# Neighbourhood attention beside a state space layer: layer 1's first block prepared in two steps a turn, and the quotients moved behind the product with the tables

## The chip, the cores and the metric

The kernel runs on one core of one Trainium2 chip. A core has five engines that work side by side, each through its own queue in order: PE (TensorE, matrix products), DVE (VectorE), ACT (ScalarE), POOL (GpSimd) and SP (SyncE, which here only issues DMA transfers). The metric is the time of one execution on the device in microseconds.

## The reference

Four layers work on an input of 4 images of 56 x 56 positions and 128 channels, all in fp32; each adds its result to its input. The change lies at the end of layer 0 and the beginning of layer 1.

```python
# layer 0: attention over a 7 x 7 neighbourhood, 4 heads of 32 channels, on group-normalised x
attn = jnp.einsum('bnijd,bnipjqd->bnijpq', q, k_win) + bias[None]
attn = jax.nn.softmax(attn.reshape(B_, nh, H_, W_, k * k), axis=-1)
out = jnp.einsum('bnijpq,bnipjqd->bnijd', attn, v_win)
return out @ w_proj + b_proj

# layer 1: two Mamba blocks on group-normalised x, over sequences of 56 positions
u = jax.nn.silu(conv(u) + cb)                      # four taps
dt, Bm, Cm = jnp.split(u @ xw, [DT_RANK, DT_RANK + D_STATE], axis=-1)
delta = jax.nn.softplus(dt @ dtw + dtb)
h = exp(delta * A) * h + delta * u * Bm            # the scan, 16 states a channel
y = sum(h * Cm) + u * D
return (y * jax.nn.silu(res)) @ ow
```

Layer 2 is an additive attention with a mixture of 64 experts behind it, layer 3 a softmax attention with a mixture of 8 experts. The change doesn't touch their code.

## The kernel before

**Layer 0.** An image is cut into 7 chunks of 8 rows (448 positions), so there are 28 chunks, numbered k from 0. Each chunk is done in two units, one for each group of column bands, so there are 56 units. A loop with a turn for each unit, and five turns more at the end, writes out the order of PE, ACT, DVE and POOL by hand. Turn i issues:

- the scores of unit i + 1 on PE (`scores`, L510), after them the steps kept in the lists `early` and `turns`;
- the weights of unit i + 1 (`weights`): exp on ACT out of PSUM (L522), then the product with the tables of the position bias (L527), three heads on DVE and one on POOL;
- the steps kept in `mid`, then the sums of unit i - 1 on PE (`sums`, L540), which gather both numerators (o) and denominators (d) of a chunk in two PSUM buffers of one copy each;
- the steps kept in `at`.

Every chunk's own work is dealt to these lists: query (`queries`, L461 and L466), key (`keys`, L471 and L475), values in two halves (`values`, L485 and L492), and the end of the chunk, `finish(k)`, in four steps. `copied` moves d and o from PSUM to SBUF on ACT (L557) and adds the projection's bias to x on POOL (L558). `divided(0)` and `divided(1)` take the reciprocal of one half of d each (L562) and multiply oT with it (L563), on DVE. `projected` is four products on PE (L568) and the sum to x on DVE (L571). The buffer d has one copy, oT two. With "end" the first turn after the chunk's own two, `copied` and `divided(0)` are in `at` of turn end, `divided(1)` in `at` of turn end + 1, `projected` in `early` of turn end + 3:

```python
for n, to, step in zip((0, 0, 1, 3), (at, at, at, early), finish(k)):
    add(end + n, step, to=to)
```

Nearly all small products (query, key, values, projection, transpositions) share one ring of two PSUM buffers, `m`; a product waits until what was there two products before has been moved out.

**The next image's norm** (`norm_steps`) is dealt over the first 12 turns of an image: seven transpositions with their statistics (L228, L238), the groups' mean and root (L245 to L273), and normalising on DVE (L285).

**Layer 1's first block.** In the last image (turns 42 to 55) the same places are taken by `next_norm`, 21 steps: seven transpositions of image 0 with statistics (n = 0 to 6), four steps to mean and root (7 to 10), `place` (11), which transposes and normalises one chunk into a room that layer 0 no longer uses (L291), and nine steps of the first Mamba block (12 to 20): two convolutions of four products each (L1012), the gate's two products (L1074) with Silu (L1025), the product with `xw` (L1031), four products that spread its rows (L1042), Softplus (L1056), the product of delta and u on POOL (L1060), and eight writes of delta and du to DRAM (L1067). The moves from PSUM are on ACT (L1020, L1082, L1037, L1048, L1053). Steps 0 to 6 come two to a turn, steps 7 to 20 one to a turn, in turns 46 to 59.

**Layer 1.** The states of 8 channels by 16 lie on the 128 partitions. SP reads delta back from DRAM, spread over the states (`fetch`, tile E, L825), ACT takes its exp (L844), PE spreads du (L806), DVE multiplies (L853) and scans (L860), POOL multiplies by C (L865), PE sums the states (L871). There are 896 scans. The tiles of layer 1 lie where tiles of layer 0 lay; a fetch waits until those are read.

Of the kernel before, what the change touches and what calls it, by code (L numbers as in the profile page):

```python
# [25 lines left out]
NCH = S // CH  # L26
# [112 lines left out]
class Hybrid:  # L139
# [215 lines left out]
    def layer0(self, wp1):  # L355
# [5 lines left out]
        with ExitStack() as ctx:  # L361
# [64 lines left out]
            def next_norm():  # L426
                g = self.first_norm = self.group_norm(0, wp1, group)
                parts = g.groups(m)
                chunk = lambda c: lambda: (g.turn(c, m), g.stats(c))
                both = lambda fs: lambda: [f() for f in fs]  # L430

                def place():
                    self.hold_block()
                    rows = self.du_room[:, : SEQ * (DC - 1 + HW)].rearrange(
                        "p (s t) -> p s t", t=DC - 1 + HW
                    )
                    nc.gpsimd.memset(rows[:, :, : DC - 1], 0.0)
                    g.chunk = lambda c: rows[:, :, DC - 1 :]
                    g.turn(0, m)
                    g.scaled(0, g.ps)  # L440
                    self.h[0, 0, 0] = rows

                s = self.first_block = self.mamba_pre(0, (0, 0, 0), None, m)
                conv = lambda f: lambda: ([s.conv(f, k) for k in range(DC)], s.conved(f))
                return [
                    *[chunk(c) for c in range(NCH)],
                    parts[0], both(parts[1:3]), both(parts[3:5]), parts[5], place,
                    conv(0), conv(1), lambda: (s.res(0), s.resed(0), s.silu("us")),
                    lambda: (s.res(1), s.resed(1)), lambda: (s.xproj(), s.dbl()),
                    lambda: (s.spread(0), s.parts(0)), lambda: (s.spread(1), s.parts(1)),  # L450
                    lambda: (s.spread(2), s.spreaded(0), s.delta()),
                    lambda: (s.du(), s.spread(3), s.spreaded(1)),
                ]
# [93 lines left out]
            def finish(k):  # L547

                b, c = chunks[k]
                x = self.X[b][:, TC * c : TC * (c + 1), :]  # L550
                r = {}

                def copied():
                    r["o"], r["d"] = self.t(sm, [P, CH], "oT"), self.t(sm, [P, CH], "d", bufs=1)
                    ps = dict(zip("od", out.pop(k)))
                    for n in "do":
                        nc.scalar.copy(r[n], ps[n][:, :CH])  # L557
                    nc.gpsimd.tensor_add(x, x, bproj.unsqueeze(1).to_broadcast([TP, TC, C]))  # L558

                def divided(n):  # L560
                    own = slice(n * 2 * TP, (n + 1) * 2 * TP)
                    nc.vector.reciprocal(r["d"][:, own], r["d"][:, own])  # L562
                    nc.vector.tensor_mul(r["o"][:, own], r["o"][:, own], r["d"][:, own])  # L563

                def projected():
                    ps = m().rearrange("p (k c) -> p k c", c=C)
                    for i in range(TC):
                        nc.tensor.matmul(  # L568
                            ps[:TP, i, :], r["o"][:, i * TP : (i + 1) * TP], wproj, start=True, stop=True
                        )  # L570
                    nc.vector.tensor_add(x, ps[:TP], x)  # L571

                return [copied, lambda: divided(0), lambda: divided(1), projected]
# [31 lines left out]
            at, mid, early, turns = {}, {}, {}, {}  # L605
            add = lambda i, f, *args, to=at: to.setdefault(i, []).append(lambda: f(*args))
# [4 lines left out]
                    add(first[NCH * (b - 1)] + n, step, to=turns if n < NCH else at)  # L611
            for n, step in enumerate(next_norm()):
                i = first[NCH * (B - 1)]
                add(i + n // 2 if n < NCH else i + n - 3, step, to=at if n % 2 and n < NCH else mid)
            for k, (b, c) in enumerate(chunks):
                i = first[k]
                end = first.get(k + 1, len(units))
                for n, to, step in zip((0, 0, 1, 3), (at, at, at, early), finish(k)):
                    add(end + n, step, to=to)
                if k >= 3:  # L620
                    add(first[k - 1] - 2 if c == 1 else first[k - 3] + (1 if c else 3), keys, k)
                if k + 1 < len(chunks):
                    add(max(i - 1, 0), queries, k + 1)
                    for half in range(2):
                        add(i + half, values, k + 1, half, to=mid)
# [1581 lines left out]
```

## Time and profile before

| What | Value |
|---|---|
| Runs of the kernel | 7031.51 us median of 3 (7016.09 to 7035.77) |
| The profiled execution's own time | 7027.59 us |
| Its span, first to last instruction | 7025.8 us |
| Busy in the span: PE, DVE, ACT, POOL | 6054.1, 5763.3, 4832.9, 2849.9 us |
| Layer 0's loop, first to last scores | 40.9 to 364.5 us |
| First scan of layer 1 | 392.1 us |
| Last scan of layer 1 | starts at 2968.0 us |
| Mean granted clock of TensorE | 0.931 |

A line of the profile's timeline gives the start in us, the duration, the engine, the line of the kernel, the operation, the tile written and the tiles read, their shapes, a count where several are merged, and in brackets how long the engine had been idle and what ended that. An entry `PE m L568` after an arrow is the instruction that was waited for. PEld is the loading of weights, which overlaps with products. A table by stages gives for each stretch its length, each engine's busy time with its number of instructions, the granted clock of TensorE, the busy share of the DMA engines and the GB/s that they moved.

### The profile page before, as it was taken

What the parts mean: (1) busy time and instruction counts of PE and PEld (TensorE: products, weight loads), DVE (VectorE), ACT (ScalarE), POOL (GpSimd) and SP (SyncE); (2) the same over time, 40 slices, a digit from 0 to 9 for tenths busy, and PEclk for the clock granted to TensorE, in tenths of its full rate; (3) what the DMA queues carried; (4) which work ended last, traced back from release to release, by engine and by line L of the source; (5) the groups of instructions that cost most, each with busy time, mean ns of one, the idle gap of its engine ahead of it and who ended that gap; (6) DMA issues with size and microseconds to landing.
All of it is one profiled execution on the core that took longest, in us unless ns stands there. A gap on an engine that the chain in (4) does not pass through costs nothing.

```text
span 7025.8 us, 101491 instructions
## 1 busy us (share of the span) xinstructions
PE 6054.1 (86%) x37386; PEld 2622.7 (37%) x37386; DVE 5763.3 (82%) x10108; ACT 4832.9 (69%) x4828; POOL 2849.9 (41%) x1921
## 2 busy tenths in 40 slices
PE   8889999999999999877777777777788799999998
PEld 7633333333233233232233323332333355555554
DVE  6879999999999999977878888888887753566665
ACT  5567667776766777589989998999899833322231
POOL 2369989998999999811010001000101100000000
PEclk9989989999999899889999999999899999999999
DMA  3057767777776777600000000000003304243433
GB/s 53 5 139 187 187 165 186 184 178 175 188 185 171 176 189 187 153 8 3 1 6 3 8 2 6 4 6 3 6 20 116 89 18 149 72 109 92 118 85 94
DMA packets 363447, 654.19 MB, mean 93 GB/s; under 512 B 95413, under 2 KB 211909, under 8 KB 362438
## 3 DMA queue, kind: packets, MB, share of 16 engines
q1 hardware_dynamic: 362949, 647.71, 36.9%
q8 instruction: 295, 4.83, 0.3%
q14 instruction: 203, 1.66, 0.1%
HBM read 536.78 MB, written 104.37 MB: 91 GB/s over the span
## 4 chain that ended last, share of the span: by engine, by line
PE 23%; ACT 12%; DVE 11%; issue 8%; POOL 1%; SPq 0%; DMA 0%; DVEq 0%; ACTq 0%; POOLq 0%
ACT th L1306 10%; PE o L1944 6%; DVE th L1297 6%; PE q L1932 5%; PE s L1320 5%; DVE X L2144 2%; PE pe L2139 2%; ACT e L1334 1%; POOL e L1341 1%; PE o L1350 1%; PE m L1478 1%; PE m L1253 1%; DVE wide L1964 1%; DVE X L1486 0%; PE m L1761 0%
## 5 line engine op out<-in xcount | busy, mean ns | idle before, releaser
L1306 ACT ACTIVATE th<-th 128x5488 f32<-128x5488 f32 (+13 forms) x560 | 2184.2, 3943 | 175.4 <-DVE th L1297 151.4
L1297 DVE TENSOR_SCALAR th<-fT,g 128x784 f32<-128x784 f32 (+13 forms) x3920 | 1868.9, 549 | 307.2 <-PE s L1320 286.5
L1320 PE MATMUL s<-th,place 128*32 128x392 f32 (+5 forms) x14112 | 1391.6, 488 | 442.2 <-ACT th L1306 439.5
L860 DVE TENSOR_TENSOR_SCAN hs<-E,u 128x896 f32<-128x896 f32 x728 | 1449.7, 2007 | 3.6 <-ACT E L844 3.6
L844 ACT ACTIVATE E<-E,rate 128x448 f32<-128x448 f32 x1456 | 886.0, 661 | 121.9 <-DMA E<-delta_dram 118.4
L865 POOL TENSOR_TENSOR hs<-hs,room 128x896 f32<-128x896 f32 x448 | 924.8, 2083 | 82.9 <-DVE hs L860 82.5
L865 POOL TENSOR_TENSOR hs<-hs,bc 128x896 f32<-128x896 f32 x448 | 926.5, 2087 | 47.3 <-DVE hs L860 45.6
L1320 PEld LDWEIGHTS s<-th,place 128*32 128x32 f32 (+1 forms) x14112 | 455.1, 111 | 1311.1 <-ACT th L1306 666.3
L1937 ACT ACTIVATE e<-q,shift 128x448 f32<-128x448 f32 (+1 forms) x511 | 322.0, 633 | 673.7 <-PE q L1932 653.4
L1341 POOL TENSOR_TENSOR e<-e,later 112x112 f32<-112x112 f32 x112 | 155.0, 1384 | 1131.4 <-ACT e L1334 676.6
L2144 DVE SCALAR_TENSOR_TENSOR X<-pe,r_gate,X 112x128 f32<-112x128 f32 x896 | 311.9, 348 | 309.6 <-PE pe L2139 273.5
L871 PE MATMUL y<-hs,sum 128*32 128x448 f32 x3584 | 499.4, 631 | 4.0 <-POOL hs L865 4.0
L1932 PE MATMUL q<-xT 128*128 128x448 f32 (+1 forms) x1022 | 501.3, 573 | 0.9 <-ACT e L1937 0.9
L1944 PE MATMUL o<-e,xk 128*128 128x448 f32 (+1 forms) x1022 | 479.2, 552 | 16.1 <-ACT oT L1909 16.1
L806 PE MATMUL u<-room,pick 32*128 32x448 f32 x1456 | 413.4, 638 | 68.5 <-DVE hs L860 66.7
L1350 PE MATMUL o<-e,xk 112*128 112x392 f32 (+5 forms) x1024 | 389.3, 500 | 91.8 <-POOL e L1341 88.2
L806 PE MATMUL u<-du,pick 32*128 32x448 f32 x1456 | 402.8, 618 | 74.2 <-DVE hs L860 72.9
L1237 POOL MEMSET xa<- 112x4 f32 (+1 forms) x32 | 55.1, 1723 | 969.9 <-PE m L1230 969.8
L853 DVE TENSOR_TENSOR u<-u,bc 128x896 f32<-128x896 f32 x364 | 391.8, 1076 | 26.1 <-PE u L806 25.8
L853 DVE TENSOR_TENSOR u<-u,room 128x896 f32<-128x896 f32 x364 | 391.8, 1076 | 22.0 <-PE u L806 21.9
L2073 POOL MEMSET lc_xa<- 112x4 f32 x28 | 3.1, 109 | 945.7 <-DVE lc_xa L2067 696.4
L848 ACT ACTIVATE u<-u 128x896 f32<-128x896 f32 x168 | 151.9, 904 | 297.3 <-PE u L797 218.1
(310 smaller groups left out, 8767.5 us busy)
## 6 DMA issues: line engine op xcount, KB each, us to landing
E<-delta_dram SPq DMA_DIRECT2D x728, 448.0 KB
V<-du_dram SPq DMA_DIRECT2D x168, 448.0 KB
wide<-in_L_ffn_weight SPq DMA_DIRECT2D x64, 1024.0 KB
r<-M SPq DMA_DIRECT2D x189, 224.0 KB
M<-wide SPq DMA_DIRECT2D x72, 392.0 KB
du_dram<-room SPq DMA_DIRECT2D x112, 112.0 KB
delta_dram<-room SPq DMA_DIRECT2D x112, 112.0 KB
du_dram<-du SPq DMA_DIRECT2D x112, 112.0 KB
```

What stands on the lines that cost most here:

```text
L806: nc.tensor.matmul(halves(to)[:, k], w["pick"][own, q, :], pre[j]["du"][own, f], start=True, stop=True,)
L844: nc.scalar.activation(e, e, AF.Exp, scale=rate)
L853: eng.tensor_mul(v, v, pre[p // PAIRS]["bc"][:, 0:1].to_broadcast([P, 2, CH]))
L860: nc.vector.tensor_tensor_scan(flat, E.pop(p), V.pop(p), 0.0, op0=ALU.mult, op1=ALU.add)
L865: nc.gpsimd.tensor_mul(HS[p], HS[p], bc[:, 1:2].to_broadcast([P, 2, CH]))
L871: nc.tensor.matmul(py[j, f][r * HD : (r + 1) * HD, :], w["sum"][:, q, :], HS[p + r // 2][:, r % 2], start=False, stop=(q == QG - 1),)
L1297: nc.vector.tensor_scalar(th[i][:, s, lo:hi], fT[j][:, lo:hi], g[b, J // WT][:, at : at + 1], None, op0=ALU.add,)
L1306: nc.scalar.activation(own, own, AF.Tanh)
L1320: nc.tensor.matmul(ps[j, J][QW * blk : QW * blk + rows, h, lo:hi], place[:, off : off + rows], z[:, at + s, h * HALF + lo : h * HALF + hi] ...
L1350: nc.tensor.matmul(po[j][:, h, lo:hi], xk[b, J // WT][:, J % WT, :], e[:, h * HALF + lo : h * HALF + hi], start=(J == 0), stop=(J == t + ( ...
L1932: nc.tensor.matmul(ps[:n, :CH], of_tile(xT[b], t), xT[b][:, c * CH : (c + 1) * CH], start=True, stop=True,)
L1944: nc.tensor.matmul(po[b, c], xk[b][:n, t, :], e[:n], start=first, stop=last)
```

## The change

All of it is where steps are put into the lists of turns. Steps 7 to 20 of layer 1's first block follow the first seven at two to a turn: even ones in `mid`, odd ones in `at`, in turns 45 to 52. And `divided(0)` goes from `at` of turn end to `mid` of turn end + 1, `divided(1)` from `at` of turn end + 1 to `mid` of turn end + 2. `copied` and `projected` keep their places. In `mid` of the last image's turns, steps of `next_norm` stand ahead of `divided`, in `at` ahead of `copied`.

```diff
             for n, step in enumerate(next_norm()):
                 i = first[NCH * (B - 1)]
-                add(i + n // 2 if n < NCH else i + n - 3, step, to=at if n % 2 and n < NCH else mid)
+                add(i + n // 2, step, to=at if n % 2 else mid)
             for k, (b, c) in enumerate(chunks):
                 i = first[k]
                 end = first.get(k + 1, len(units))
-                for n, to, step in zip((0, 0, 1, 3), (at, at, at, early), finish(k)):
+                for n, to, step in zip((0, 1, 2, 3), (at, mid, mid, early), finish(k)):
                     add(end + n, step, to=to)
```

No instruction is added to or taken from the program but what the places imply: the order on each engine, the waits, and on ACT the loads of function tables between functions of different sets.

## The prediction

> **What bounds the kernel now.** I read the table of busy time by stage first. The three stretches are a middle piece of layer 0, loop turns 46 to 53, and the passage into layer 1.
>
> ```profile
> core 0: us, PE busy (x) PEld busy (x) DVE busy (x) ACT busy (x) POOL busy (x), PEclk, DMA share, GB/s
> 200.00:280.00 80.00, 69.83 (x1370) 55.92 (x1366) 63.68 (x86) 47.89 (x79) 31.04 (x21) 0.99 0.02 6
> 318.56:363.97 45.41, 43.06 (x798) 32.96 (x797) 32.07 (x40) 30.61 (x47) 17.40 (x13) 1.00 0.01 3
> 363.97:392.10 28.13, 24.13 (x246) 13.14 (x242) 14.32 (x16) 13.14 (x20) 7.00 (x7) 0.88 0.28 71
> ```
>
> In layer 0, PE works 87% and then 95% of the stretch: it is the bound, and what counts is what it waits for. Its waits come from the timeline. This is one pair of turns, from one even scores product (L510) to the next, with the same place of the following pair last:
>
> ```profile
> 234.94 0.86 PE L510 MATMUL s<-q,kT 32*112 32x112 f32 x24
> ...
> 237.34 1.21 DVE L527 TENSOR_TENSOR e<-e,tab 112x1008 f32<-112x1008 f32 x1 [0.34 <-ACT e L522]
> ...
> 238.93 0.54 ACT L557 COPY d<-d 128x448 f32<-128x448 f32 x1
> ...
> 239.47 1.13 PE L568 MATMUL m<-wproj,oT 128*112 128x128 f32 x8
> 239.50 1.55 DVE L562 RECIPROCAL d<-d 128x224 f32<-128x224 f32 x1 [0.94 <-ACT d L557]
> ...
> 241.66 0.68 DVE L571 TENSOR_TENSOR X<-m,X 112x512 f32<-112x512 f32 x1
> ...
> 242.41 0.91 PE L485 MATMUL m<-wqkv,room 128*112 128x128 f32 x6 [1.43 <-DVE X L571]
> ...
> 246.68 0.86 PE L510 MATMUL s<-q,kT 32*112 32x112 f32 x24
> ...
> 252.16 0.82 PE L485 MATMUL m<-wqkv,room 128*112 128x128 f32 x6
> ```
>
> The projection (239.47) waits for nothing. Its sum (241.66) sits on DVE behind the next chunk's quotient (239.50), and PE waits 1.43 us for it, because a transposition stands between projection and values and the two-buffer ring m comes round. In the next pair nothing stands between, and values start at once (252.16). At the image's last turns another wait shows:
>
> ```profile
> 285.39 0.54 ACT L557 COPY d<-d 128x448 f32<-128x448 f32 x1
> ...
> 286.23 0.66 ACT L475 ACTIVATE kT<-m,bqkv 128x448 f32<-128x448 f32 x1
> ...
> 286.94 1.09 PE L510 MATMUL s<-q,kT 32*112 32x104 f32 x32 [1.02 <-ACT kT L475]
> ```
>
> The next image's first scores wait for keys that ACT moves only behind the denominators' copy. Last, the passage:
>
> ```profile
> 363.97 0.86 PE L510 MATMUL s<-q,kT 32*112 32x112 f32 x24
> ...
> 382.51 0.34 SPq L1067 DMA_DIRECT2D du_dram<-room  x1
> ...
> 386.40 1.29 SPq L825 DMA_DIRECT2D E<-delta_dram  x2
> ...
> 390.84 1.23 ACT L844 ACTIVATE E<-E,rate 128x448 f32<-128x448 f32 x2 [6.97 <-DMA E<-delta_dram]
> ...
> 392.10 2.02 DVE L860 TENSOR_TENSOR_SCAN hs<-E,u 128x896 f32<-128x896 f32 x1 [1.76 <-ACT E L844]
> ```
>
> From the last unit's scores to layer 1's first scan are 28.1 us; from 500 us on DVE is busy 59.5 of 60 us. So a later or earlier scan shifts the end by as much.
>
> **What the Trainium skill says.** PSUM — Partial Sum Buffer, "Engine vs sequencer instructions": the queues of ScalarE, VectorE and GpSimdE are strict FIFO. The trace agrees: the kT copy at 286.23 stands behind the d copy. ScalarE: Activation LUTs, "What ACT_TABLE_LOAD costs", states about 1283 ns for a load and more for a drain; the trace has 1.28 us, with the next function 1.3 us after the load's start, so I price 1.3. TensorE: Matmul & The Clock Gate, "What's actually happening": an idle PE falls to half clock. The trace agrees: four L1012 take 3.35 us at 381.94 and 1.77 at 386.48. SBUF — State Buffer, "SBUF: two separate sides", says that a GpSimd instruction and a DVE one with two SBUF inputs block each other for a whole instruction. The trace agrees: the same table product takes 2.31 us at 314.16, with POOL's part running from 313.99 for 1.06, and 1.54 at 219.28, after POOL's had ended. So part of DVE's sums can come 0.8 us later than I count.
>
> **The change, part by part.** T is the start of an even scores product; durations are the trace's.
>
> *Quotients.* The number of instructions stays. In order of DVE it was: table product, first half of quotient k, sum k-1, table product, second half. It becomes: table product, second half of k-1, sum k-1, table product, first half of k. What is late next:
>
> (a) The second half of the projection now needs exp (ends T+2.3), table product (T+2.4 to 3.6), reciprocal and product (1.94): T+5.55. PE gets there at T+4.5 and fills 0.55 with the first half. It resumes at 5.65, and behind it on PE stand values, sums, query and key; the sum ends at 7.0; values with a transposition before them start at 7.05 instead of 7.47: -0.4. There are 7 such pairs: -2.8. Without a transposition values start at T+6.2 and not 5.48: +0.75, in 3 pairs: +2.25. The pair with the statistics' second matmul, which waited for the sum too (265.10), breaks even.
>
> (b) d has one buffer. Copying denominators k on ACT must now wait for the second half of k-1: T+5.6, not T+4.0. Behind it on ACT stand the copy of oT, the next exp and the moves of v and q. In a plain pair exp then ends at 8.4 instead of 6.6, while the next scores come at 11.7: hidden; with less than 3.3 us of cover each us would cost one. At the image's end it is not hidden: DVE is behind with normalising (1.88 and 1.44). Counting DVE from 271.3: 1.95 quotient, 5.0 root and normalising, 0.4, 0.7 sum, 1.55, 1.95, 1.44, 0.4, table product to 285.8, second half to 287.75. Copies d and oT to 288.9, kT to 289.55: scores at 289.6 instead of 286.94: +2.7, three times: +8.1.
>
> (c) In turns 42 to 45 of the last image two transpositions fall in a turn. Half a quotient now stands between two statistics that free m: 15.0 instead of 13.1 us and 13.4 instead of 12.35: +2.9.
>
> *First block.* 14 steps move from turns 46 to 59 into turns 45 to 52. PE: two convolutions of 3.2, two L1074 of 0.9, L1031 1.77, four L1042 of 1.0. Of these 6.7 us came behind the last scores and now come ahead of them. ACT: the moves of these products (0.55 to 0.65 each), Silu 0.96, Softplus 0.95, and one more return to the exp table, 1.3. POOL: 2.07 + 0.3, in turn 52; its 17.4 us busy of 45 hide it (otherwise 2.4). SP: eight writes, 3.6 us, on a queue that is idle there; the fetches behind them wait for buffers of layer 0 anyway. I set the durations one behind another in queue order:
>
> - Turns 46-47 take 15.9 us (before 11.15). The square root waits for the second statistics behind a quotient (6.5); then copies 1.1, exp table 1.3, exp to 10.85, table product to 12.5, root to 14.1, the normalised chunk to 14.9. Keys need its m buffer: to 15.85.
> - Turns 48-49: 18.3 (before 9.66). PE alone: 9.4 of usual work with key and query, 6.5 and 1.8 of the block; the wait for m behind Silu and its table is 0.65.
> - Turns 50-51: 15.9 (before 12.11). PE 13.3: 8.5 of usual work, 1.8 and three times 1.0; then scores wait 2.6 for q, which stands on ACT behind the move of bc, table and Softplus (12.4 to 15.2), then 0.65.
> - Turns 52-53: 9.5 (before 12.49): 7.6 without key and query, 1.0, and 0.75 to 0.9 of wait (a).
>
> Together 59.6 against 45.4: +14.2.
>
> *Passage.* From the last scores: table product to 3.6, second half of 25 to 5.55, copies of 26 to 6.7, sum 25 to 7.0, quotient 26 to 10.9, copies of 27 to 12.05, sum 26 to 12.3, quotient 27 to 16.2, projection and sum to 17.7. First convolution and spread inputs to 18.7, again to 20.6, two DVE products to 21.8: scan. E, fetched once the last sums end (9.6) and landing 4.4 later as before, is there by 14. At half clock the scan comes at 25.7; I take 23.8: -4.3. The five first scans spread over 15.8 us before, as PE stood behind a move that waited on ACT for E (392.64 after 386.48). With E there I count 11.3 at full clock; half clock eats about 1: -3.5.
>
> Sum: -2.8 + 2.25 + 8.1 + 2.9 + 14.2 - 4.3 - 3.5 = +16.8. The profiled execution took 7027.6 (span 7025.8): 7044.4. The median of the runs is 3.9 above it: 7048. The count of turns 46 to 49 puts every wait in a row; I take 2 off for overlap that I cannot place: **7046 us**.
>
> **Rivals.** *Waits absorbed, faster.* The four pairs from turn 46 on have about 1.5 us each of the wait for the sum, and the moved work falls into it: +0.7 instead of 14.2. With no loss at the image ends: -2.8 + 2.25 + 0.7 - 6.3 - 4.5 = -10.7: 7021. For it speaks the wait of 1.43; against it PE's 43.06 of 45.41. *ACT late in every pair, slower by over 0.3%.* If exp behind the held copy ends later than the 3.3 us of cover allow, from about T+11.7 on, each of some 24 pairs pays; at 0.8 us each: +19 over my sum, 7065. Against it: in the pairs at 246 ACT is idle 2.2 us before the query. *Only the passage matters, nothing else moves:* -7.8 + 6.7: 7030, no change; against it, the kT wait exists already. *The change does nothing* is excluded: the queues' orders differ.
>
> **How the numbers follow.** About 0.3% (21 us) is what a measurement of this kernel can tell from no change: 7010 to 7053. My sum's case has 0.58, its own range 7036 to 7058; absorbed 0.17; ACT late 0.15; passage only 0.10. Within my case 0.18 lie above 7053, with the ACT case 0.33 slower. Faster by over 21 us needs the absorbed case and 10 us more: 0.09. Range: 7022 to 7066, the ends of the two rivals.
>
> **What would show it.** Right: L568's second half waits for L563; the d copy waits for L563 in nearly every chunk; first scores of images 1 to 3 late behind kT by some 2.7 us more; q behind Softplus; E landed before ACT asks; the last scores some 25 us later and the first scan some 20. Wrong: the pairs from turn 46 sum to under 52 us, or plain pairs grow by over 0.5 us.

## The result, and the profile after

| | Kernel before | Changed kernel |
|---|---|---|
| Median of the runs | 7028.11 us (7016.09 to 7035.77) | 7055.39 us (7051.73 to 7061.11) |
| Ratio, with its 95% interval | | 1.0041 (1.0028 to 1.0054) |
| Span of the profiled execution | 7025.8 us | 7049.9 us |
| Mean granted clock of TensorE | 0.931 | 0.931 |

The changed kernel is slower by 27 us. The forecast was 7046 us in a range from 7022 to 7066: 14.5 us over the median of three runs that it started from, and 18 us over the median here.

Each profile shows one execution, which need not take the median time (the changed kernel's took 7051.73 us). Cut by the starts of scores products (L510) and of the first scan, the two profiled executions compare so:

| Stretch | Before, us | After, us | Difference | Forecast |
|---|---|---|---|---|
| Start of turn 2's scores | 60.31 | 58.13 | -2.2 | none |
| Turns 2 to 41 | 232.78 | 253.01 | +20.2 | +7.55 |
| Turns 42 to 45 | 25.47 | 26.30 | +0.8 | +2.9 |
| Turns 46 to 53 | 45.41 | 65.66 | +20.25 | +14.2 |
| Last scores to first scan | 28.13 | 26.65 | -1.5 | -4.3 |
| First scan starts at | 392.10 | 429.75 | +37.65 | +20.35 |
| Last scan starts at | 2968.0 | 2996.2 | +28.2 | +16.8 |

Forecast +7.55 is the sum of its terms -2.8, +2.25 and +8.1. Of the 37.65 us, 9.4 come back between the first scan and the last, and another 4 behind the last, so that the spans differ by 24.1. The question of this document is why both places where the forecast put a loss lost more than it said: about 13 us more in turns 2 to 41 and 6 more in turns 46 to 53.

The table by stage of the changed kernel, with the same columns as before: length, busy time by engine with the number of instructions, and then the clock granted to PE.

```profile
core 0: us, PE busy (x) PEld busy (x) DVE busy (x) ACT busy (x) POOL busy (x), PEclk, DMA share, GB/s
58.13:311.14 253.01, 213.71 (x3961) 170.09 (x3960) 184.48 (x252) 139.63 (x230) 102.27 (x60) 0.94 0.03 6
337.44:403.10 65.66, 55.89 (x812) 39.22 (x811) 34.61 (x41) 38.21 (x57) 24.44 (x16) 0.90 0.06 16
403.10:429.75 26.65, 18.68 (x235) 12.87 (x232) 16.60 (x18) 6.77 (x12) 4.64 (x5) 0.86 0.25 67
```

In turns 46 to 53 PE has 14 instructions more than before (812 against 798). They are large products of layer 1's first block: its 32 products in these turns take 15.6 us, and the 18 before took 7.4. But PE's busy time grows by more than that, from 43.06 to 55.89 us, at a clock of 0.90 instead of 1.00, and its idle time from 2.35 to 9.8 us. So PE has more to do, waits more, and does a part of its work more slowly.

An ordinary pair of turns in the timeline of the changed kernel, which answers to the first pair shown of before (T is 223.26):

```profile
223.26 0.86 PE L510 MATMUL s<-q,kT 32*112 32x112 f32 x24
...
227.59 1.26 POOL L558 TENSOR_TENSOR X<-X,bproj 112x512 f32<-112x512 f32 x1
...
228.37 0.74 DVE L563 TENSOR_TENSOR oT<-oT,d 128x224 f32<-128x224 f32 x1
...
229.16 0.69 PE L568 MATMUL m<-wproj,oT 128*112 128x128 f32 x4 [0.69 <-DVE oT L563]
229.21 0.53 ACT L557 COPY d<-d 128x448 f32<-128x448 f32 x1 [1.86 <-DVE oT L563]
...
230.70 0.91 PE L485 MATMUL m<-wqkv,room 128*112 128x128 f32 x6 [0.47 <-DVE X L571]
```

What the forecast named is there. Two waits are new: the second half of the projection (229.16) and the copy of the denominators (229.21) wait for the quotient's product. The wait for the sum (230.70) has shrunk from 1.43 to 0.47 us. The values start at T + 7.44; before it was T + 7.47. In such a pair the change moves the wait and doesn't shorten it.

The end of the third image, at the place shown of before (there the scores waited 1.02 us and took 1.09):

```profile
299.69 0.72 DVE L563 TENSOR_TENSOR oT<-oT,d 128x224 f32<-128x224 f32 x1
...
300.52 0.53 ACT L557 COPY d<-d 128x448 f32<-128x448 f32 x1 [2.55 <-DVE oT L563]
...
301.37 0.65 ACT L475 ACTIVATE kT<-m,bqkv 128x448 f32<-128x448 f32 x1
302.07 1.92 PE L510 MATMUL s<-q,kT 32*112 32x104 f32 x32 [3.67 <-ACT kT L475]
303.92 2.05 PE L568 MATMUL m<-wproj,oT 128*112 128x128 f32 x8
```

The first four lines are the whole chain: product, copy of d, move of kT, and scores for which PE waits 3.67 us. Behind the wait the scores take 1.92 us and not 1.09, the projection (303.92) 2.05 and not 1.13: the granted clock was 0.50 from 302 to 307 us.

In turns 52 and 53 a wait stands that the forecast had two turns earlier and in another form:

```profile
387.72 1.28 ACT L1056 ACT_TABLE_LOAD   x1
...
390.50 1.28 ACT L522 ACT_TABLE_LOAD   x1
...
393.25 1.21 DVE L527 TENSOR_TENSOR e<-e,tab 112x1008 f32<-112x1008 f32 x1 [4.86 <-ACT e L522]
...
395.18 2.06 POOL L1060 TENSOR_TENSOR room<-room 128x896 f32<-128x896 f32 x1
...
395.95 1.53 DVE L563 TENSOR_TENSOR oT<-oT,d 128x224 f32<-128x224 f32 x1
...
397.54 1.20 PE L568 MATMUL m<-wproj,oT 128*112 128x128 f32 x4 [2.65 <-DVE oT L563]
```

Two loads of function tables hold exp, exp holds the table product, and the second half of the quotient now stands behind that product. Then its multiplication takes 1.53 us and not 0.39, as POOL's product of delta and u runs at the same time. PE waits 2.65 us, and its clock over these two turns is 0.80.

The passage, from last scores at 403.10:

```profile
410.50 0.53 ACT L557 COPY d<-d 128x448 f32<-128x448 f32 x1 [4.75 <-DVE oT L563]
...
417.64 1.23 ACT L844 ACTIVATE E<-E,rate 128x448 f32<-128x448 f32 x2
...
422.80 0.69 DVE L571 TENSOR_TENSOR X<-m,X 112x512 f32<-112x512 f32 x1 [1.35 <-PE m L568]
...
429.75 2.01 DVE L860 TENSOR_TENSOR_SCAN hs<-E,u 128x896 f32<-128x896 f32 x1
```

E is there before ACT asks for it (417.64, no wait), where before, the first scan waited 1.76 us for ACT's exp of it. What is late is the last sum: it ends at T + 20.4, before at T + 17.05.

### The profile page after: what moved, and what is told of

It reads as the page before. It is cut to its first block, busy times and chain, and to the rows that moved or that the text cites. A ratio compares the mean times of both kernels' runs of the same rounds, so it can differ in the third digit from the quotient of the medians.

```text
span 7049.9 us, 101456 instructions
## 1 busy us (share of the span) xinstructions
PE 6059.2 (86%) x37386; PEld 2631.4 (37%) x37386; DVE 5760.3 (82%) x10108; ACT 4833.3 (69%) x4828; POOL 2869.0 (41%) x1921
## 4 chain that ended last, share of the span: by engine, by line
PE 22%; ACT 12%; DVE 11%; issue 9%; POOL 1%; SPq 0%; DMA 0%; DVEq 0%; ACTq 0%; POOLq 0%
ACT th L1306 10%; PE o L1944 6%; DVE th L1297 6%; PE q L1932 5%; PE s L1320 4%; PE pe L2139 2%; DVE X L2144 2%; ACT e L1334 1%; POOL e L1341 1%; PE o L1350 1%; PE m L1478 1%; PE m L1253 1%; DVE wide L1964 1%; DVE X L1486 0%; PE m L1761 0%
## 5 line engine op out<-in xcount | busy, mean ns | idle before, releaser
L853 DVE TENSOR_TENSOR u<-u,room 128x896 f32<-128x896 f32 x364 | 391.5, 1076 | 11.7 <-PE u L806 11.7
```

The lines of the kernel that those rows point to most:

```text
L853: eng.tensor_mul(v, v, pre[p // PAIRS]["bc"][:, 0:1].to_broadcast([P, 2, CH]))
```

## The experiments

The theory behind the forecast, called A: the two parts cost separately. The quotients lose because the one buffer of d makes the denominators' copy, and the keys behind it, wait; the block loses because its products come on PE ahead of the last scores, where PE is the bound. Its rivals: one part carries all of the loss, or a late quotient costs in any place, with any number of buffers.

**The block alone.** The first changed line without the second.

```diff
-                add(i + n // 2 if n < NCH else i + n - 3, step, to=at if n % 2 and n < NCH else mid)
+                add(i + n // 2, step, to=at if n % 2 else mid)
```

> Only the steps of layer 1's first block come two to a turn; the quotients stay where they were. Theory A (two costs that add up: in the traces the quotients lost about 20 us up to turn 44 and the block about 20 us from turn 46 to 53, of which the passage into layer 1 gave back 9 to 11): 8 us slower than before, 3 to 14; the image ends (turns 12, 26 and 40) as before, the pairs 46 to 53 together 12 to 20 us longer, the first scan 10 to 19 us later. Rival B (the block carries the whole loss): 25 us slower. Rival C (the loss needs both edits, since the held copy of the denominators and the loads of function tables meet in the same turns): within 3 us of before.

Measured: 7036.83 us (7026.31 to 7043.93) against 7027.72, ratio 1.0014 (1.0006 to 1.0022): +9 us. Turns 46 to 53 take 58.42 us (+13.0), the passage 27.19 (-0.9), the first scan comes 10.5 us later. So neither does the block carry the whole loss, nor does the loss need both parts. The table by stage of this kernel, turns 46 to 53 and then the passage:

```profile
316.97:375.39 58.42, 52.71 (x811) 38.37 (x810) 30.86 (x36) 38.23 (x57) 18.33 (x15) 0.94 0.02 4
375.39:402.58 27.19, 19.36 (x235) 12.96 (x232) 19.76 (x20) 6.87 (x12) 7.71 (x7) 0.81 0.43 106
```

PE's busy time in the passage falls from 24.13 to 19.36 us, and the passage gets shorter by 0.9. The work that was taken out of it had cost next to nothing there: behind the last scores PE has 4 to 8 us of idle time, since the chain of quotients, projections and sums is longer than its own work. Ahead of the last scores the same work costs more than its length: PE's busy time grows by 9.65 us (about 7 of them the block's products, the rest a clock of 0.94 and not 1.00), its idle time by 3.4.

**The quotients alone.** The second changed line without the first.

```diff
-                for n, to, step in zip((0, 0, 1, 3), (at, at, at, early), finish(k)):
+                for n, to, step in zip((0, 1, 2, 3), (at, mid, mid, early), finish(k)):
```

> Only the quotients are moved behind the product with the tables; layer 1's first block stays at one step a turn. Theory A: 20 us slower than before, 15 to 25, of which 13 to 15 at the three image ends, where keys wait on ACT behind the held copy of the denominators; the passage into layer 1 as before within 4 us. Rival B (the block carries the whole loss): within 3 us of before. Rival C (needs both): under 8 us slower.

Measured: 7054.01 us (7048.15 to 7059.64), ratio 1.0039 (1.0026 to 1.0051): +26 us, just over what theory A expected. Turns 2 to 41 take 251.99 us (+19.2, of which 14.0 in the pairs at the three image ends), turns 46 to 53 52.79 (+7.4), the passage 32.33 (+4.2). So nearly the whole loss of the changed kernel comes with this part alone. +9 and +26 don't add up to +27: with late quotients the passage grows by 4.2 us as long as the block stands in it, and moving the block out takes that back (26.65 in the changed kernel). That is about half of the gap; the other half comes back between the first scans, which the section on the prediction takes up.

**A second buffer for half of d.** The changed kernel, with d as two tiles for the two halves, of which the later has two copies. The copy from PSUM then needs two instructions, and, to make room, a temporary of the position bias's tables is put where weights `e` will lie later; of the edit, only the tiles are shown.

```diff
-                    r["o"], r["d"] = self.t(sm, [P, CH], "oT"), self.t(sm, [P, CH], "d", bufs=1)
+                    r["o"] = self.t(sm, [P, CH], "oT")
+                    r["d"] = [self.t(sm, [P, 2 * TP], f"d{n}", bufs=1 + n) for n in range(2)]
```

> The kernel after, with the denominators in two tiles of half a chunk, the second of them in two buffers, so that copying them never waits for the quotient of the chunk before (the copy is two instructions instead of one, and the scratch of the bias tables lies in another tile to make room; nothing else differs). If the one buffer causes most of the quotients' loss (theory A): 12 to 18 us faster than after, 7038 to 7044, image ends back to within 1.5 us of before; the pairs without a transposition stay 0.7 to 1 us longer, since the projection still waits for the second half. If the loss comes from the projection's wait for the second half instead (rival D): within 4 us of after.

Measured: 7039.58 us (7033.02 to 7044.96), ratio to before 1.0018 (1.0010 to 1.0025), 16 us under the changed kernel. Turns 2 to 41 take 233.45 us, 0.7 over before. The waits of the scores for keys, as total, number and longest in us, are in this kernel

```profile
PE s L510 <- ACT kT L475: 3.2, 3, 1.1
```

and in the kernel before

```profile
PE s L510 <- ACT kT L475: 3.1, 3, 1.0
```

Turns 46 to 53 still take 64.57 us. So the one buffer is the cause of the net loss in turns 2 to 41, and it is not the cause of what the quotients lose in turns 46 to 53. The pairs without a transposition stay 0.94 us longer, as the projection still waits for the second half.

**The block spread more evenly.** The kernel before, with steps 7 to 20 over ten turns (46 to 55): between its place before, in 14 turns, and after, in 8.

```diff
-                add(i + n // 2 if n < NCH else i + n - 3, step, to=at if n % 2 and n < NCH else mid)
+                turn = i + n // 2 if n < NCH else i + 4 + (n - NCH) * 9 // 13
+                add(turn, step, to=at if (n % 2 if n < NCH else n in (8, 11, 14, 17)) else mid)
```

> The kernel before, with steps 7 to 20 of layer 1's first block spread over turns 46 to 55 instead of 46 to 59 (never more than two in a turn, and the two convolutions in different turns). If the loss of the block is its packing into five turns of layer 0 and the gain at the passage is its being ready (theory A): 3 to 8 us faster than before, the first scan up to 8 us earlier. If any step taken out of the passage costs as much ahead of it (rival E, PE bound there): within 3 us of before.

Measured: 7034.02 us (7025.93 to 7038.62), ratio 1.0007 (0.9999 to 1.0015). The first scan comes at 402.4, as with the block alone, and turns 46 to 53 take even longer, 62.68 us; the passage takes 23.96. Theory A had expected 3 to 8 us of gain: no gain is shown, and a small loss is not excluded. So the packing into few turns is not shown to be what costs. A gentler pace moves the time between the two stretches, but not the sum (86.6 us against 85.6 with the block alone and 73.5 before).

**Only the first half of the quotient moved.** The kernel before, with the second half left in `at` of turn end + 1.

```diff
-                for n, to, step in zip((0, 0, 1, 3), (at, at, at, early), finish(k)):
+                for n, to, step in zip((0, 1, 1, 3), (at, mid, at, early), finish(k)):
```

> The kernel before with only the first half of each quotient moved (to `mid` of turn end + 1); the second half stays in `at` of turn end + 1, so the one d buffer is free before the next denominators' copy comes. Theory A (the change's quotients lose through the one d buffer, which only the second half's new place touches): no loss; and since the sum of the projection no longer stands behind the next chunk's first half on DVE, the values wait less: in the profile VALUES (L485) wait for the sum 5 us in layer 0 instead of 14.6, and the median is 6 to 18 us under before (7010 to 7022). Rival (later quotients lose in any place, since the projection comes to wait for them): the projection's second half waits 1 us or more in each pair and the time is 5 to 15 above before.

Measured: **7013.40 us** (7008.93 to 7025.54) against 7026.84, ratio 0.9983 (0.9976 to 0.9990): 13 us under before, the fastest of all. Turns 2 to 41 take 223.21 us (-9.6). The timeline of this kernel, in a pair whose T is 216.55:

```profile
221.07 1.13 PE L568 MATMUL m<-wproj,oT 128*112 128x128 f32 x8
...
222.31 0.69 DVE L571 TENSOR_TENSOR X<-m,X 112x512 f32<-112x512 f32 x1 [1.05 <-PE m L568]
...
223.06 0.91 PE L485 MATMUL m<-wqkv,room 128*112 128x128 f32 x6 [0.47 <-DVE X L571]
```

The projection waits for nothing, and the sum starts the moment that its products are done: DVE has been idle for 1.05 us, where before it was in the next chunk's reciprocal. The values start at T + 6.5 and not T + 7.47, and their waits for the sum in layer 0 fall from 14.6 to 5.0 us, as expected. The copy of d doesn't have to wait here, as both halves are divided well before it comes.

**Only the second half moved.**

```diff
-                for n, to, step in zip((0, 0, 1, 3), (at, at, at, early), finish(k)):
+                for n, to, step in zip((0, 0, 2, 3), (at, at, mid, early), finish(k)):
```

> The kernel before with only the second half of each quotient moved (to `mid` of turn end + 2); the first half stays in `at` of turn end. Theory A: nearly all of the quotients' loss comes with this half, as the denominators' copy must wait for it: 15 to 27 above before (7043 to 7055), with the copy (L557) waiting for the product (L563) in nearly every chunk and the first scores of images 1 to 3 waiting 4 to 6 us each for keys. Rival (the halves share the loss): 8 to 14 above before, and the rest with the first half.

Measured: 7087.04 us (7084.16 to 7096.32), ratio 1.0082 (1.0068 to 1.0096): +60 us, twice what theory A had expected at most. The timeline of this kernel shows what the expectation left out, in a pair whose T is 270.93:

```profile
276.88 0.53 ACT L557 COPY d<-d 128x448 f32<-128x448 f32 x1 [1.86 <-DVE oT L563]
...
277.45 1.55 DVE L562 RECIPROCAL d<-d 128x224 f32<-128x224 f32 x1 [0.68 <-ACT d L557]
...
279.62 0.68 DVE L571 TENSOR_TENSOR X<-m,X 112x512 f32<-112x512 f32 x1
...
280.36 1.62 PE L485 MATMUL m<-wqkv,room 128*112 128x128 f32 x6 [2.45 <-DVE X L571]
```

The late second half delays the copy of d on ACT; the next chunk's first half, still in its old place, stands on DVE waiting for that copy; behind it stands the sum, and behind the sum the values on PE. Such a ring over three engines closes in all seven pairs with a transposition: in this one the wait for the sum grows from 1.43 to 2.45 us. In five of the seven the values then run near half of their speed before (1.62 us and not 0.91), and the seven take 3.3 to 5.0 us more each. At the image ends the scores wait 3.3 to 3.9 us for keys, less than the 4 to 6 expected, and the three pairs there grow by 7.7 us of the 44 by which turns 2 to 41 grow. So theory A named the right half, but its size fell, since it had left out the ordinary pairs. The two moves are no two small effects that add: the first alone gains 13 us, the second alone loses 60, and with the second done the first saves 30 to 34 of those.

**The block with the first half.** The changed kernel with the second half put back.

```diff
-                for n, to, step in zip((0, 1, 2, 3), (at, mid, mid, early), finish(k)):
+                for n, to, step in zip((0, 1, 1, 3), (at, mid, at, early), finish(k)):
```

> The changed kernel with the second half of each quotient put back to `at` of turn end + 1: the block's new places and the first half's new place together. If costs add, this is the first half's own effect (theory A: 6 to 18 under before) and the block's +9: 7018 to 7030. If the block's places gain once the quotients don't stand in their way, it is under the run with the first half alone.

Measured: 7023.40 us (7016.88 to 7031.73), ratio 0.9995 (0.9987 to 1.0003): 10 us over the run with the first half alone. The time is that of the kernel before: the interval includes no change. Turns 46 to 53 take 57.28 us against 45.56 in the run with the first half alone. The block's new places cost about the same with either order of the quotients, so long as the second half isn't late. Turns 52 and 53 take 9.63 us, as with the block alone (9.62); in the changed kernel they take 15.09.

**Keys ahead of the copy.** The changed kernel, with the keys of each next image's second chunk first in the list `at` in which they stood behind the copy of d.

```diff
-                if k >= 3:
-                    add(first[k - 1] - 2 if c == 1 else first[k - 3] + (1 if c else 3), keys, k)
+                if k >= 3 and c == 1:
+                    at.setdefault(first[k - 1] - 2, []).insert(0, lambda k=k: keys(k))
+                elif k >= 3:
+                    add(first[k - 3] + (1 if c else 3), keys, k)
```

> The changed kernel with one edit: the next image's second chunk's keys, which were put behind the copies of denominators in `at` of the turn two ahead of the image's end, stand first in that list, so ACT moves them before it copies d. If the three waits of 4 to 6 us at the image ends are the step of the prediction that was too small (+2.7 each, measured +4.1 to +5.0), the time falls by 10 to 14 us against the changed kernel (7041 to 7046) and the first scores of images 1 to 3 wait 1 us or less for keys. Rival: the copy of d only reaches PE by another way there (the projection, the values), and the time falls by less than 5.

Measured: 7040.85 us (7034.86 to 7050.07), ratio to before 1.0020 (1.0013 to 1.0027), 14.5 us under the changed kernel. What PE waits for in layer 0, as total, number and longest wait in us; first the changed kernel:

```profile
PE m L568 <- DVE oT L563: 25.0, 20, 3.8
PE s L510 <- ACT kT L475: 14.8, 3, 5.9
```

and then this one:

```profile
PE m L568 <- DVE oT L563: 29.3, 22, 3.8
...
PE s L510 <- ACT kT L475: 2.2, 3, 0.7
```

The three waits for keys shrink from 14.8 to 2.2 us, and the time falls by about as much, while the larger total of twenty-two waits for the quotient stays. In ordinary pairs those waits stand in place of others; at the image ends the wait for keys came on top.

## Why the prediction was right or wrong

The direction, the mechanism and most of the named waits were right; the loss was 27 us and not 14.5 to 18. That the number came so near is in part luck. The forecast took it that a later first scan shifts the end by as much, and counted 3.5 us back. The first scan came 37.65 us later and not 20.35, and the last scores 39.1 us later and not some 25; then 13.5 us came back behind the first scan. Two errors of some 17 and 10 us stood against each other. By its own steps:

- **(a) the projection waits for the second half.** Right in its place, 0.2 to 0.4 us off in size in each pair but one. Six of the seven pairs with a transposition gain 0.03 to 0.15 us and not 0.4: the multiplication, taken at 0.39 us, lasts 0.74 beside POOL's sum of the bias. The seventh, turns 4 and 5, loses 2.0: two waits of 0.69 and 1.12 us follow each other there, and PE falls to a clock of 0.57 behind them. So the seven together lost 1.5 us, where a gain of 2.8 had been counted. The pairs without a transposition lose 0.93 to 1.03 us, and 0.75 had been said. "Plain pairs grow by over 0.5 us" had been named as a sign against, and it didn't say which pairs it meant, so it can't be counted either way.
- **(b) one d buffer.** The mechanism is shown twice, by the second buffer and by the keys put ahead. This is the term that was mis-sized most: +2.7 at each image's end, and the pairs of turns there grew by 4.9, 5.0 and 4.1. At the third the wait for keys is 3.67 us, 2.65 over before and so as counted; what the sum lacked there is the half clock behind it, 0.83 us more on the scores and 0.92 on the projection alone. At the first two the wait was longer too (5.9 and 5.2 us), and no run here shows why these two differ from the third: all three together are 14.8 us against 3.1 before, 11.7 more and not 8.1.
- **(c) turns 42 to 45.** +2.9 was said, +0.8 measured: that half a quotient between two statistics would hold the ring was over-sized.
- **First block.** For turns 46 to 53, 59.6 us had been counted; the block alone takes 58.4. The term was good as a count of the block. It held 0.75 to 0.9 us for the late quotients, and the changed kernel takes 7.2 us over the block alone. Most of that is in turns 52 and 53 (15.09 us, where 9.5 had been counted and the block alone takes 9.62). The step that failed is the 2.6 us of wait for q behind Softplus in turns 50 and 51. Softplus ended when the forecast said, but the q behind it on ACT is wanted one turn later than I had taken, so turns 50 and 51 took 13.2 us instead of 15.9. Softplus, its load of tables and the load back to exp's hold exp of the next turn, and with it the table product and the second half behind it. With the second half put back, turns 52 and 53 take 9.63.
- **Passage.** -4.3 was said, -1.5 measured. The end behind the last sum was right (6.1 us counted, 6.3 measured). The chain ahead of it was counted at 17.7 us and took 20.4: the first table product took 1.94 and not 1.21, the product of the quotient behind it 1.09 and not 0.39, both beside POOL: 1.4 of the 2.7 us. The Trainium skill, SBUF — State Buffer, "SBUF: two separate sides", says that such pairs exclude each other for a whole instruction. The trace agrees: the multiplications of 0.74, 1.09 and 1.53 us all end 0.24 to 0.26 us behind the end of POOL's instruction. The forecast had cited the page, and then priced every DVE instruction as if alone.
- **First scans.** -3.5 was said for the first five, and it is -3.3: they spread over 12.5 us. But another 7.2 us come back up to the sixteenth scan, for which there was no step: the first sixteen take 46.6 us and not 57.2, and DVE waits less for the spread inputs from PE (from the sixth scan on 2.1 us and not 8.1). The sixteen take 51.8 us with the block alone and 58.4 with the quotients alone, but also 46.6 with the block spread more evenly, where the quotients stand as before. So the late quotients aren't needed for it; why these orders differ stays open. Open too are the 4 us behind the last scan. The 2.2 us by which layer 0's loop began earlier need no cause: in the ten profiles turn 2 begins between 57.6 and 61.5 us.
- **The rivals.** "Waits absorbed" fell. It counted on about 1.5 us of wait in each of the four pairs from turn 46 on, but PE was idle for only 2.35 us in all four together. Moving the first half alone does shorten the wait for the sum and gives 7013, but by clearing DVE's order, not by filling the wait. "ACT late in every pair" fell: in the ordinary pair shown exp ends at T + 8.5, and the next scores come at T + 11.7. "Only the passage" fell with the table of stretches.

## What to carry to other kernels

When an instruction is put later in an engine's order, ask of its input's buffer who writes it next, and what stands behind that writer on its own engine: here a copy, then keys, then the next image's first products. Split a move into its halves before judging it; one half of this one gains 13 us and the other turns it into a loss. And before work is pulled ahead of a stretch's end, look whether the stretch it leaves was limited by that work at all: this passage was limited by a chain of quotients, and got 0.9 us shorter for 4.8 us of PE's busy time taken out.

## What the runs showed of the hardware

- A short wait can cost PE more than itself. With waits of 0.69 and 0.47 us in an ordinary pair PE stayed at full clock (1.00 from 229 to 233 us; six products in 0.91 us). With waits of 0.69 and 1.12 us the granted clock was 0.57 from 76 to 80 us, and the same products took 1.62. A single wait of 1.43 us in the kernel before left it at 1.00. The Trainium skill, TensorE: Matmul & The Clock Gate, "What's actually happening", ties half clock to an idle window of about 3.4 us. Here PE had been busy for 1.9 of the 3.4 us before the clock fell at 76.2 us, so idle time in pieces was enough. Whether the length of the waits decides or where they fall isn't shown: in the kernel before, PE was busy for 2.0 of the 3.4 us up to 242.4 us, and the clock stayed at 1.00.
- DVE's multiplication of half a chunk took 0.39 us in most places, 0.72 to 0.74 beside POOL's bias sum of 1.26, and 1.53 beside POOL's product of 2.06 us.
